# Graph products and transposes as two half-array products per 128 rows, in a four-layer graph network on one core

## The chip, the cores and the metric

The kernel runs on one core of a Trainium2 chip. The metric is the device time of one execution in microseconds (us): 2440.18 us, the median of three runs (2438.67 to 2441.17). All tensors are float32.

## The reference

`x` is 128 batches of 64 nodes of 256 features; `adj` is one 64 x 64 graph, with its own diagonal, for all batches. Four layers follow each other, each of the form `x = layernorm(x + layer(x))`:

```python
# layer 0: normalized graph product, two dense layers with batch norm
agg = einsum('nm,bmd->bnd', A_hat, x)
out = bn(relu(bn(agg @ W1.T + b1)) @ W2.T + b2)
# layer 1: graph product with the scaled Laplacian, attention of 4 heads over the graph, MLP
h  = relu(layernorm(einsum('mn,bnf->bmf', L_norm, x) @ Wc + bc)); x1 = h + x
o  = softmax(mask(q k^T / 8)) v          # q, k, v = x1 @ Wq, Wk, Wv; 4 heads of 64
x2 = layernorm(x1 + o @ Wo + bo); out = layernorm(x2 + gelu(x2 @ W1 + b1) @ W2 + b2)
# layer 2: two graph convolutions, then LSTMs over windows of 1, 2, 3 and 4 nodes
h = relu(adj @ (x @ Wg0 + bg0)); h = relu(adj @ (h @ Wg1 + bg1)); h = lstm_windows(h)
# layer 3: graph attention with additive scores
Wh = x @ W; e = leaky_relu(Wh @ a1 + (Wh @ a2)^T); out = softmax(mask(e)) @ Wh
```

## The kernel before, in words

The 128 batches are cut into 16 blocks of 8 batches. A block is a tile of 128 partitions by 1024 columns and has two layouts. In the row layout (`tm`) the 128 partitions are two batches of 64 nodes, and the columns are 4 such pairs (`t`, `NT` = 4) of 256 features. In the feature layout (`fm`) the partitions are 128 features and the columns are two feature chunks (`c`) of 512 rows each. Everything of eight batches is thus eight squares of 128 x 128.

Work arrives at TensorE (PE) as groups, each of which fills one of four PSUM tiles `ps0` to `ps3`. Such a tile is 128 x 1024 float32 and covers two PSUM banks of 512 columns (`TB`). ScalarE (ACT) or VectorE (DVE) then copies the tile out, often with an addition or an activation in the same instruction, and gives it back. The groups that matter here:

- `aggregate` (L318-328, the product at L322) multiplies a block in the row layout by the graph and leaves it in the feature layout: 8 products, in which the block's square of 128 x 128 is the stationary operand and a 128 x 128 matrix, block diagonal with the graph twice, is the moving one. It is called once per block in layer 0 (`first_block`, with `AhT`), once in layer 1 (`block`, with `LnT`) and twice in layer 2 (`gcn_block`, with `bdAT`): 64 calls.
- `to_fm` (L330, the transposes at L334) and `to_tm` (L336, L340) change the layout with PE transposes of 128 x 128 against `ident`. `block` calls `to_fm` twice, `end_block` calls `to_tm` once, and `last_block` calls each once. The last four blocks are dealt with in two halves there.
- In `block`, the attention: `q` and `k` come from `mm_fm` (L346), `v` from L705; the scores (L730) are 32 products of 64 x 64 by 64 x 64; their softmax is transposed by eight squares (L764); attention times `v` (L778) is again 32 products of 64 x 64 by 64 x 64, whose outputs of head parity `r` go to partition half `r`.
- Dense products: `mm_fm` (L346), `mm_tm` (L358), L566, L835; the LSTM products are at L952, L1024, L1161 and L1163.

The columns of `Wq`, `Wk`, `Wv` are the four heads in turn, 64 each; head 2u + r lies in chunk `u`, half `r`. L609 loads each of these weights with one DMA from SyncE's queue (SP), early in the program.

The order of work on every engine is fixed when the program is written. `flow` (L126) plays a list scheduler: each task is a generator that yields `step(engine, us, ...)` with an estimated time, and `flow` always takes the step that can begin first, by those estimates, with a priority among streams and a count of free PSUM tiles (`PS`) and SBUF tiles (`mem`). The estimate for an aggregation is 1.8, for a transposing group 0.9, for the scores 1.8, for attention times v 2.0, for a dense group 3.45. On the chip each engine then runs its own list in order and waits on semaphores.

Of the kernel before, what the change touches and what calls it, by code (L numbers as in the profile page):

```python
# [33 lines left out]
def kernel(ctx: ExitStack, tc: tile.TileContext, a: dict, out: bass.AP):  # L34
# [267 lines left out]
    def ln_steps_act(y):  # L302
# [10 lines left out]
        for t in range(n):  # L313
            S.activation(  # L314
                y[:, t, :], y[:, t, :], AF.Identity, scale=rs[:, t : t + 1], bias=nm[:, t : t + 1]
            )

    def aggregate(ps, y, mT):  # L318

        for c in range(2):  # L320
            for t in range(NT):
                T.matmul(  # L322
                    ps[:, c, t * P : (t + 1) * P],
                    y[:, t, c * P : (c + 1) * P],
                    mT,
                    start=True,
                    stop=True,
                )

    def to_fm(ps, y):  # L330

        for c in range(2):
            for t in range(y.shape[1]):
                T.transpose(ps[:, c, t * P : (t + 1) * P], y[:, t, c * P : (c + 1) * P], ident)  # L334

    def to_tm(ps, yT):  # L336

        for t in range(ps.shape[1]):
            for c in range(2):
                T.transpose(ps[:, t, c * P : (c + 1) * P], yT[:, c, t * P : (t + 1) * P], ident)  # L340

# [45 lines left out]
    with c0:  # L387
# [135 lines left out]
        def first_block(i):  # L523
# [4 lines left out]
            else:  # L528
                xs = early[i]
            yield step("T", 1.8, ps=1, sl=1)  # L530
            ps = PS.take()
            ag = mem.take()
            aggregate(fm(PS[ps]), tm(mem[xs]), AhT)
            mem.give(xs)
            yield step("V", 1.25, ps=-1)
            aggT = fm(mem[ag])
            V.tensor_copy(aggT, fm(PS[ps]))
            PS.give(ps)
# [69 lines left out]
        for k, w in zip(("Wc", "Wq", "Wk", "Wv", "Wo", "W1", "W2"), (Wc, Wq, Wk, Wv, Wo, W1, W2)):  # L608
            nc.sync.dma_start(w, by_chunk(a[f"L1_gnn_{k}"]))  # L609
        names = ("bc", "g1", "be1", "bo", "g2", "b2", "g3", "be3")  # L610
# [20 lines left out]
    def end_block(i):  # L631
        x = X[i]
        yield step("Q", 6.0, sl=1)
        xin = mem.take()
        nc.sync.dma_start(tm(mem[xin]), x_blk[i])
        yield step("S", 1.4)
        for c in range(2):
            S.activation(
                H[i][:, c, :], H[i][:, c, :], AF.Identity, scale=sc2[:, c : c + 1], bias=sh2[:, c : c + 1]
            )  # L640
        yield step("T", 0.9, ps=1)
        ps = PS.take()
        to_tm(tm(PS[ps]), H[i])
        mark("h", i)
        yield step("V", 1.25, ps=-1)
        V.tensor_tensor(x, tm(PS[ps]), tm(mem[xin]), ALU.add)
        PS.give(ps)
        mem.give(xin)
        yield from ln_steps_act(x)
        mark("end", i)  # L650

    def block(i):
        x = X[i]
        mark("begun", i)
        yield step("T", 1.8, ps=1, sl=1)
        ps = PS.take()
        s_xp = mem.take()
        aggregate(fm(PS[ps]), x, LnT)
        yield step("S", 1.05, ps=-1)
        S.copy(mem[s_xp], PS[ps])  # L660
        PS.give(ps)
# [12 lines left out]

        yield step("T", 0.9, ps=1, sl=1)
        ps = PS.take()
        s_x1 = mem.take()
        to_fm(fm(PS[ps]), y)
        yield step("S", 1.05, ps=-1)
        x1T = fm(mem[s_x1])  # L680
        S.copy(mem[s_x1], PS[ps])  # L681
        PS.give(ps)
# [42 lines left out]
        pq = PS[ps].rearrange("p (r g m) -> p r g m", r=2, g=8)  # L725
        for b in range(8):
            t, s = b // 2, b % 2
            for u in range(2):
                for r in range(2):
                    T.matmul(  # L730
                        pq[s * N : (s + 1) * N, r, 2 * t + u, :],
                        qT[r * N : (r + 1) * N, u, b * N : (b + 1) * N],
                        kT[r * N : (r + 1) * N, u, b * N : (b + 1) * N],
                        start=True,
                        stop=True,
                    )
        for j in qk:
# [20 lines left out]

        yield step("T", 0.9, ps=1, sl=1)
        ps = PS.take()  # L760
        s_a = mem.take()
        pt = PS[ps].rearrange("p (g m) -> p g m", g=8)
        for g in range(8):
            T.transpose(pt[:, g, :], e[:, g, :, :].rearrange("p r m -> p (r m)"), ident)  # L764
        mem.give(s_e)
        yield step("S", 1.05, ps=-1)
        aT = mem[s_a].rearrange("p (g m) -> p g m", g=8)
        S.copy(mem[s_a], PS[ps])
        PS.give(ps)
        yield step("T", 2.0, ps=1, sl=1)  # L770
        ps = PS.take()
        s_o = mem.take()
        po = fm(PS[ps])
        for b in range(8):
            t, s = b // 2, b % 2
            for u in range(2):
                for r in range(2):
                    T.matmul(  # L778
                        po[r * N : (r + 1) * N, u, b * N : (b + 1) * N],
                        v[r * N : (r + 1) * N, b, u, :],  # L780
                        aT[r * N : (r + 1) * N, 2 * t + u, s * N : (s + 1) * N],
                        start=True,
                        stop=True,
                    )
# [14 lines left out]

        yield step("T", 0.9, ps=1, sl=1)  # L800
        ps = PS.take()
        s_x2 = mem.take()
        to_fm(fm(PS[ps]), y)
        yield step("S", 1.4, ps=-1)
        x2T = fm(mem[s_x2])
        for c in range(2):
            S.activation(
                x2T[:, c, :], fm(PS[ps])[:, c, :], AF.Identity, scale=g2c[:, c : c + 1], bias=be2c[:, c : c + 1]
            )
# [393 lines left out]
    def gcn_block(i):  # L1203
        yield step("T", 1.8, ps=1, sl=1)
        ps = PS.take()
        s_a = mem.take()
        aggregate(fm(PS[ps]), X[i], bdAT)
        yield step("Q", 4.0, waits=False)
# [3 lines left out]
        yield step("S", 1.05, ps=-1)  # L1212
        S.copy(mem[s_a], PS[ps])
        PS.give(ps)
# [10 lines left out]
        S.activation(mem[s_h1], mem[s_h1], AF.Relu)  # L1225
        yield step("T", 1.8, ps=1, sl=1)
        ps = PS.take()
        s_a = mem.take()
        aggregate(fm(PS[ps]), h1, bdAT)
        mem.give(s_h1)  # L1230
        yield step("S", 1.05, ps=-1)
        S.copy(mem[s_a], PS[ps])
        PS.give(ps)
# [119 lines left out]
    def last_block(i, t0=0, nt=NT):  # L1353
# [9 lines left out]
        for c in range(2):  # L1363
# [3 lines left out]
            )  # L1367
        yield step("T", 0.9 * r, ps=1)
        ps = PS.take()
        px = tm(PS[ps])[:, :nt, :]  # L1370
        to_tm(px, hb)
        mem.give(s_h)
        mark("read", i)
        yield step("V", 0.1 + 1.2 * r, ps=-1)
        V.tensor_tensor(x, px, x, ALU.add)
        PS.give(ps)
        yield from ln_steps_act(x)

        yield step("T", 0.9 * r, ps=1, sl=1)
        ps = PS.take()  # L1380
        s_xT = mem.take()
        px = fm(PS[ps])[:, :, : nt * P]
        to_fm(px, x)


        yield step("S", 0.3 + 1.1 * r, ps=-1)
        xT = fm(mem[s_xT])[:, :, : nt * P]
        pairs, into = (ap.rearrange("p c (u e k) -> p c u e k", e=2, k=P) for ap in (px, xT))
        S.copy(into[:, :, :, 0], pairs[:, :, :, 0])
        for h in range(2):  # L1390
            S.copy(into[:, :, :, 1, halves[1 - h]], pairs[:, :, :, 1, halves[h]])
        PS.give(ps)
# [243 lines left out]
```

## Time and profile before

| | us |
|---|---|
| median of three runs | 2440.18 |
| the profiled execution | 2439.17 |
| span of its records | 2437.4 |
| PE busy | 2348.3 |
| DVE busy | 1215.1 |
| ACT busy | 1169.9 |
| POOL busy | 566.7 |
| PE, all aggregations (L322) | 130.8 |
| PE, all transposes of `to_fm`, `to_tm` (L334, L340) | 94.4 |
| PE, attention times v (L778) | 33.1 |

The span is what the records of the program cover; the execution's own time is 1.8 us longer. A product of float32 leaves two pairs of records, each a LDWEIGHTS (engine PEld, the stationary operand) and a MATMUL (engine PE, the moving operand): the 128 aggregating products with `AhT` have 256 MATMUL records. A transpose leaves one pair. In a row, `64*64 64x64` says that the stationary operand has 64 partitions by 64 columns and that the output is 64 partitions by 64 columns. [...] The granted clock of PE was 0.983 over the span.

### The profile page before, as it was taken

The numbers are of one execution on the slowest core, as the hardware profiler recorded it, in microseconds if no ns is written. First come the engines' busy times: TensorE is split into PE (matmuls) and PEld (weight loads), VectorE is DVE, ScalarE is ACT, GpSimd is POOL, SyncE is SP. The second block draws the span as 40 slices with busy tenths as digits, with TensorE's granted clock in tenths as the row PEclk, the third lists the DMA queues.
The fourth block names the chain that finished last, engine by engine and source line by source line (L and its number), as shares of the span: only waits on it lengthen the run. The fifth ranks groups of instructions, "written<-read, shape, count | busy, mean of one in ns | idle before, by whom it ended". The sixth has DMA issues, their size and how long they took to land. (4 is left out here: it accounts for less than half of the span.)

```text
span 2437.4 us, 33965 instructions
## 1 busy us (share of the span) xinstructions
PE 2348.3 (96%) x13700; PEld 1798.9 (74%) x13700; DVE 1215.1 (50%) x2864; ACT 1169.9 (48%) x2138; POOL 566.7 (23%) x426
## 2 busy tenths in 40 slices
PE   8999889999999999999999999999999999998997
PEld 5544567766676666676676788899999888887785
DVE  4542377646475345744462433344435444455446
ACT  2255453543444444335544444444444654468766
POOL 0000034222333222422231221222212222122112
PEclk9999989999999999999999999999999999999998
DMA  5110111000000000000010000000001000001111
GB/s 172 44 52 0 40 31 49 27 9 10 1 10 18 10 9 10 1 10 34 20 61 1 18 1 1 1 18 1 1 1 35 1 9 10 18 27 66 40 35 44
DMA packets 40974, 57.47 MB, mean 24 GB/s; under 512 B 4592, under 2 KB 33904, under 8 KB 40816
## 3 DMA queue, kind: packets, MB, share of 16 engines
q1 hardware_dynamic: 39712, 54.22, 6.9%
q8 instruction: 107, 1.75, 0.3%
q10 hardware_dynamic: 1104, 1.08, 0.1%
q14 instruction: 51, 0.42, 0.1%
HBM read 38.52 MB, written 16.78 MB: 23 GB/s over the span
## 5 line engine op out<-in xcount | busy, mean ns | idle before, releaser
L1024 PE MATMUL ps<-x,x 128*128 128x256 f32 x1024 | 248.6, 380 | 0.7 <-DVE t L1092 0.7
L1024 PEld LDWEIGHTS ps<-x,x 128*128 128x128 f32 x1024 | 191.5, 190 | 26.4 <-issue 1.6
L314 ACT ACTIVATE x<-x,ln_nm,ln_rs 128x256 f32<-128x256 f32 x196 | 103.7, 592 | 97.0 <-DVE ln_nm L311 95.5
L1024 PE MATMUL ps<-t,x 128*128 128x256 f32 x576 | 141.0, 379 | 0.0
L308 POOL TENSOR_TENSOR ln_rs<-ln_rs,neghalf 128x4 f32<-128x4 f32 (+1 forms) x72 | 70.5, 980 | 231.1 <-DVE ln_rs L274 217.3
L1024 PEld LDWEIGHTS ps<-t,x 128*128 128x128 f32 x576 | 108.6, 190 | 14.6 <-issue 0.4
L346 PE MATMUL ps<-t,W1T 128*128 128x512 f32 x256 | 115.2, 593 | 0.0
L952 PE MATMUL ps<-h,wL 128*128 128x192 f32 (+2 forms) x504 | 111.6, 375 | 0.0
L952 PEld LDWEIGHTS ps<-h,wL 128*128 128x128 f32 x504 | 79.1, 190 | 27.6 <-issue 26.7
L272 DVE BATCH_NORM_STATS2 ln_st<-x 128x6 f32<-128x256 f32 x256 | 98.2, 404 | 0.5
L1100 ACT ACTIVATE t<-t,bih 128x512 f32<-128x512 f32 (+2 forms) x63 | 41.0, 652 | 107.6 <-DVE t L1090 105.9
L952 PE MATMUL ps<-h,x 128*128 128x256 f32 x384 | 86.8, 379 | 0.0
L964 ACT ACTIVATE t<-ps,bih 128x512 f32<-128x512 f32 (+3 forms) x104 | 61.5, 642 | 44.0 <-PE ps L952 43.9
L294 POOL TENSOR_TENSOR ln_rs<-ln_rs,neghalf 128x4 f32<-128x4 f32 x32 | 36.9, 1153 | 188.8 <-DVE ln_rs L274 188.6
L346 PEld LDWEIGHTS ps<-t,W1T 128*128 128x128 f32 x256 | 46.3, 190 | 46.4 <-issue 46.4
L952 PEld LDWEIGHTS ps<-h,x 128*128 128x128 f32 x384 | 72.9, 190 | 10.3 <-issue 0.5
L1083 DVE COPY t<-ps 128x256 f32<-128x256 f32 (+2 forms) x63 | 23.7, 378 | 113.5 <-PE ps L1024 113.5
L273 DVE BATCH_NORM_AGGREGATE ln_mv<-ln_st 128x2 f32<-128x6 f32 x448 | 71.3, 167 | 0.0
L346 PE MATMUL ps<-t,wA 128*128 128x512 f32 x144 | 67.9, 617 | 2.8 <-ACT t L681 2.8
L952 PE MATMUL ps<-t,wL 128*128 128x512 f32 x144 | 64.9, 607 | 2.5 <-ACT t L1250 2.5
L1090 DVE TENSOR_TENSOR t<-ps,t 128x512 f32<-128x512 f32 (+2 forms) x63 | 38.1, 604 | 54.8 <-PE ps L1024 47.9
L1100 ACT ACTIVATE x<-x,bih 128x512 f32<-128x512 f32 (+2 forms) x57 | 36.6, 641 | 55.7 <-DVE x L1090 55.4
(692 smaller groups left out, 5688.2 us busy)
## 6 DMA issues: line engine op xcount, KB each, us to landing
t<-in_x_dram SPq DMA_DIRECT2D x26, 512.0 KB, 3.9
xd<-x SPq DMA_DIRECT2D x16, 512.0 KB, 2.6
x<-xd SPq DMA_DIRECT2D x6, 512.0 KB, 3.3
out_dram<-x SPq DMA_DIRECT2D x6, 512.0 KB, 3.0
wL<-in_L_gnn_Wih_dram SPq DMA_DIRECT2D x2, 1024.0 KB, 4.9
h<-in_x_dram SPq DMA_DIRECT2D x4, 512.0 KB, 4.2
x<-in_L_gnn_Whh_dram SPq DMA_DIRECT2D x2, 1024.0 KB, 4.9
t<-xd SPq DMA_DIRECT2D x4, 512.0 KB, 3.3
```

What stands on the lines that cost most here:

```text
L272: V.bn_stats(st[:, t, :], y[:, t, :])
L273: V.bn_aggr(mv[:, t, :], st[:, t, :])
L294: G.tensor_tensor(rs, rs, neghalf[:, :NT], ALU.pow)
L308: G.tensor_tensor(rs, rs, neghalf[:, :n], ALU.pow)
L314: S.activation(y[:, t, :], y[:, t, :], AF.Identity, scale=rs[:, t : t + 1], bias=nm[:, t : t + 1])
L346: T.matmul(ps[:, c, :], w[:, k, (off + c) * P : (off + c + 1) * P], yT[:, k, :], start=(k == 0), stop=(k == nk - 1),)
L952: T.matmul(spread(fm(PS[ps])[:, j, :n], q), WL[p][0][:, k, m], x_of(0, q)[:, k], start=(k == 0), stop=(k == 1),)
L964: S.activation(of(sl)[:, j], fm(PS[ps])[:, j, :n], AF.Tanh if g == 2 else AF.Sigmoid, bias=bias(g, c))
L1024: T.matmul(dst, WS[p][name](k, g), y[:, k], start=first and k == 0, stop=k == 1, skip_group_check=not first)
L1083: V.tensor_copy(y[:, 1, :], v[:, 0, :])
L1090: V.tensor_tensor(y[:, 0:2, :], v[:, 2:4, :], y[:, 0:2, :], ALU.add)
L1100: S.activation(of(act[g])[:, 0], of(act[g])[:, 0], f, bias=bias(g, 0))
```

## The change

The two batches of a square are no longer kept apart by zeros in a 128 x 128 matrix. Each aggregating product becomes two, one per batch: the stationary operand is 64 partitions (one half `h` of `halves`) by 128 columns, the moving one the 64 x 64 graph in the same partitions. The same is done with all transposes, against a 64 x 64 piece of `ident`. The two products of a pair write to the two banks of the PSUM tile (`part`), and the copy out joins them again (`joined` reads the banks in turn in runs of 64 columns, `runs` names the destination in the same shape). In attention times v the four combinations of head parity and `u` go to four different quarters of the array, so that heads 2 and 3 change places in the output; the columns of `Wq`, `Wk` and `Wv` are loaded in that order, which takes three DMAs per weight. The score products come in another order. The estimates of the steps concerned are lowered.

```diff
+    def part(ps, s, g):
+        return ps[:, s * TB + g * N : s * TB + (g + 1) * N]
+    def joined(ps, n=2 * NT):
+        return ps.rearrange("p (s g e) -> p g s e", s=2, e=N)[:, :n]
+    def runs(ap):
+        if len(ap.shape) == 2:
+            return ap.rearrange("p (g s e) -> p g s e", s=2, e=N)
+        return ap.rearrange("p t (c s e) -> p (t c) s e", s=2, e=N)
...
     def aggregate(ps, y, mT):
         for c in range(2):
             for t in range(NT):
-                T.matmul(
-                    ps[:, c, t * P : (t + 1) * P],
-                    y[:, t, c * P : (c + 1) * P],
-                    mT,
-                    start=True,
-                    stop=True,
-                )
+                for s, h in enumerate(halves):
+                    T.matmul(
+                        part(ps, s, c * NT + t),
+                        y[h, t, c * P : (c + 1) * P],
+                        mT[h, h],
+                        start=True,
+                        stop=True,
+                    )
     def to_fm(ps, y):
...
-            for t in range(y.shape[1]):
-                T.transpose(ps[:, c, t * P : (t + 1) * P], y[:, t, c * P : (c + 1) * P], ident)
+            for t in range(n):
+                for s, h in enumerate(halves):
+                    T.transpose(part(ps, s, c * n + t), y[h, t, c * P : (c + 1) * P], ident[h, h])
...
-            yield step("T", 1.8, ps=1, sl=1)
+            yield step("T", 0.95, ps=1, sl=1)
...
-            V.tensor_copy(aggT, fm(PS[ps]))
+            V.tensor_copy(runs(mem[ag]), joined(PS[ps]))
...
+            if k in ("Wq", "Wk", "Wv"):
+                for m, j in ((slice(0, P), slice(0, P)), (slice(P, P + N), slice(P + N, 2 * P)), (slice(P + N, 2 * P), slice(P, P + N))):
+                    nc.sync.dma_start(w[:, :, m], src[:, :, j])
...
-        S.copy(mem[s_xp], PS[ps])
+        S.copy(runs(mem[s_xp]), joined(PS[ps]))
...
-        for b in range(8):
-            t, s = b // 2, b % 2
+        for t in range(NT):
             for u in range(2):
-                for r in range(2):
+                for s in range(2):
+                    b = 2 * t + s
+                    for r in range(2):
...
-        yield step("T", 0.9, ps=1, sl=1)
+        yield step("T", 0.5, ps=1, sl=1)
...
         for g in range(8):
-            T.transpose(pt[:, g, :], e[:, g, :, :].rearrange("p r m -> p (r m)"), ident)
+            for s, h in enumerate(halves):
+                T.transpose(part(PS[ps], s, g), mem[s_e][h, g * P : (g + 1) * P], ident[h, h])
...
-        yield step("T", 2.0, ps=1, sl=1)
+        yield step("T", 1.3, ps=1, sl=1)
...
-                        po[r * N : (r + 1) * N, u, b * N : (b + 1) * N],
-                        v[r * N : (r + 1) * N, b, u, :],
-                        aT[r * N : (r + 1) * N, 2 * t + u, s * N : (s + 1) * N],
+                        po[halves[r ^ u], u, b * N : (b + 1) * N],
+                        v[halves[r], b, u, :],
+                        aT[halves[r], 2 * t + u, s * N : (s + 1) * N],
```

The other copies out of aggregations and transposes change as the two shown do; `to_tm` changes as `to_fm`. In `last_block` the copy after `to_fm`, three ACT instructions before (L1389, L1391), becomes two.

## The prediction

> **What bounds the kernel now.** I read the page first: the busy times and the slices. PE is busy 96% of the span in nearly every slice; VectorE and ScalarE are at half. A change of PE work therefore counts almost in full, and a slower copy out of PSUM mostly doesn't.
>
> ```profile
> PE 2348.3 (96%) x13700; PEld 1798.9 (74%) x13700; DVE 1215.1 (50%) x2864; ACT 1169.9 (48%) x2138; POOL 566.7 (23%) x426
> ...
> PE   8999889999999999999999999999999999998997
> ```
>
> Next came the groups by line and shape, for the paces of the products that the change touches and of those that already use half of the array's rows (busy, then mean of one).
>
> ```profile
> L764 PE MATMUL ps<-ident,t 128*128 128x128 f32 x64 | 8.3, 273 | 0.0
> L778 PE MATMUL ps<-h 64*64 64x64 f32 x64 | 2.1, 220 | 0.0
> L730 PE MATMUL ps<-t,x 64*64 64x64 f32 x64 | 1.2, 222 | 0.0
> ```
>
> With 64 records and both less one record: L778 goes at (2.1 - 0.22) / 63 = 30 ns a record, L730 at (1.2 - 0.22) / 63 = 15.6 ns. The first has two quarters of the array in use, so one quarter starts a record each 59 ns; the second has four, and the same pace per quarter. Quarters thus run side by side, and 59 ns is the price of one record with 64 columns loaded and 64 streamed.
>
> The timeline gives the full-array groups.
>
> ```profile
> 424.50 1.84 PE L905 MATMUL ps<-av,t 128*128 128x1 f32 x16
> ...
> 431.51 1.04 PE L764 MATMUL ps<-ident,t 128*128 128x128 f32 x8
> ...
> 704.26 1.95 PE L322 MATMUL ps<-bdAT,h 128*128 128x128 f32 x16
> ```
>
> The aggregation goes at (1.95 - 0.275) / 15 = 112 ns a record, a transpose at (1.04 - 0.273) / 7 = 110 ns. L905 decides what the change is worth: its products stream one column, against 128 of L322, and still start (1.84 - 0.25) / 15 = 106 ns apart. It isn't the streaming that holds them but the loading of 128 columns of weights. The weight loads of four lines, minimum, median and maximum in ns, say what that load depends on:
>
> ```profile
> L905 PEld LDWEIGHTS ps<-av,t x16: 190/192/192, 424.3 to 426.1; 128*128 128x128 f32 x16
> ...
> L705 PEld LDWEIGHTS ps<-wA,t x576: 132/137/138, 324.9 to 1074.3; 128*64 128x64 f32 x192
> ...
> L778 PEld LDWEIGHTS ps<-h x64: 129/135/135, 354.3 to 356.1; 64*64 64x64 f32 x64
> ...
> L764 PEld LDWEIGHTS ps<-ident,t x64: 139/141/146, 365.9 to 1141.7; 128*128 128x128 f32 x64
> ```
>
> 64 columns take 137 ns from 128 rows and 135 ns from 64: rows don't matter. 128 columns take 192 ns, 55 to 57 ns more. But 128 columns of a transpose (L764) take 141 ns, like 64 of a product.
>
> Last I looked at the borders between groups with the whole array and groups in quarters.
>
> ```profile
> 781.15 0.59 PE L346 MATMUL ps<-t,wB 128*128 128x512 f32 x1
> 781.68 0.27 PE L730 MATMUL ps<-t,x 64*64 64x64 f32 x2
> ...
> 781.68 1.21 PE L730 MATMUL ps<-t,x 64*64 64x64 f32 x64
> 782.82 0.33 PE L334 MATMUL ps<-ident,t 128*128 128x128 f32 x1
> ...
> 661.12 1.21 PE L730 MATMUL ps<-t,h 64*64 64x64 f32 x64
> 662.26 0.38 PE L322 MATMUL ps<-LnT,x 128*128 128x128 f32 x1
> ```
>
> From end to end: L346 ends at 781.74 and the first scores at 781.95, 0.21 us later where 0.06 is their pace: 0.15 lost. The scores end at 782.89 and the next transpose at 783.15, 0.26 against 0.11: 0.15 lost. Where an aggregation follows (662.33 to 662.64) it is 0.31 against 0.11: 0.20 lost. Full-array groups that follow each other lose nothing: L322 above starts 0.43 us after the last 512-column product, which is that product's own pace. So each change of the array's shape empties it and shows the first load: 0.15 us where that load is short (64 columns, or a transpose), 0.20 us where a product loads 128 columns.
>
> **The change part by part.**
>
> Aggregations, 64 groups. Before, 16 records in a row at 112 ns: 1.79 us. After, 32 records in two halves, 16 in each: the stationary operand has 64 rows and still 128 columns, so each half is held by the same load, 16 x 112 ns = 1.79 us. Gain: none. The trace has no half of 64 rows by 128 columns, so the ends are the pace of a 64-column record, 16 x 59 ns = 0.94 us (64 x 0.85 = 54 us gained), and halves that don't overlap at all, 3.58 us (115 us lost). I take no gain, since the row nearest to it, L905, has the same load with less streaming; the loss I give hardly a chance, because L730's four quarters load side by side.
>
> [...]
>
> Transposes, 768 of them, 96 groups of eight (the halves of `last_block` counted as halves). Before 8 x 110 ns = 0.88 us; after 8 in each half at 59 ns = 0.47 us, since their load is short. Gain 96 x 0.41 = 39 us. The ends: this, and no gain, if the short load isn't to be had in half of the rows (8 x 112 = 0.90 us).
>
> Attention times v, 16 groups of 64 records, from two quarters to four: 63 x (30 - 15.6) ns = 0.91 us each, 14.5 us. The scores already go at the pace of four quarters: nothing.
>
> Borders. I counted them in the order in which PE's instructions stand in both programs. Before, the shape of the array changes 151 times, 94 of them into a short load and 57 into a long one: 94 x 0.15 + 57 x 0.20 = 25.5 us. After it changes 340 times, 148 and 192: 60.6 us. Loss 35 us. That the shape of 64 rows by 128 columns costs the same per border as the quarters is taken over from the rows above; at nothing for it the loss would be 0, at twice the price 70.
>
> Copies out. They read the two banks in turn, in runs of 64. The nearest rows: ACT's L1391 (256 columns in runs of 64) takes 392 ns against 365 to 377 for plain 256-column copies (L1062, L1064), so 0.1 us more at most for 1024 columns; DVE's L1242 in runs of 64 takes 678 ns for 512 columns against 688 plain at L1090. 168 copies by 0.1 us are 17 us at worst, hidden behind PE's 96%; without that cover they are lost. The copy in `last_block` loses one instruction (585 + 2 x 392 ns to 2 x 585), 0.2 us of ACT, also hidden.
>
> DMAs. Wq, Wk and Wv take nine issues on SP for three, six more of 0.5 to 1.4 us (L609's rows), 3 to 8 us between 12 and 29 us. Behind them on SP wait the other weights, the `rows` and the load of the eighth block of x, issued at 28.6 us before. PE needs that block only after seven blocks of layer 0, each 1.8 + 2 x 3.4 = 8.7 us, so about 60 us after its start at 8; the weights are first used at 297 us. Cost nothing; at most 8 us if that slack weren't there.
>
> Sum: 35 - 39 - 14.5 = -18.5 us. Profiled span 2437.4 - 18.5 = 2418.9; the execution was 1.8 us longer than its span, and the median of the runs 1.0 above that execution: 2421.7. I predict 2421 us.
>
> **The rivals.**
>
> Aggregations are halved as well. For it: two halves would stream 64 columns each. Against it: L905. Then 2421 - 54 = 2367 us.
>
> Transposes don't get faster, so the change is slower. The place is the load of a transpose in 64 rows: L764 has its 141 ns in a full array, and the program's other transposes of halves (L1450) are written as plain products, which is no proof of either. If the load takes what a product's takes, the 39 us are gone, 1.5 us are lost (8 x 112 ns against 0.88), and some 100 of the borders cost 0.20 instead of 0.15, 5 us: 2421 + 46 = 2467 us. It decides from the point where a transposing pair takes more than about 90 ns, since 96 x 8 x 24 ns eat the 18.5 us.
>
> The fixed order turns bad. `flow` now plans 0.95 us for an aggregation that by my sum takes 1.8 plus two borders, 2.2 us; 64 x 1.2 = 79 us of PE work that ACT's and DVE's lists don't reckon with. Before, its 1.8 matched. PE's waits are now 2437 - 2348 = 89 us. A fifth more of them, 18 us, and the gain is gone; with a third more, 2421 + 30 = 2451 us. Against it: a PE that is later than planned finds its inputs ready.
>
> **How the numbers follow.** From one measurement to the next some 0.2% (4.9 us) can't be told from no change. My forecast has 0.52, with its own range 2405 to 2437 (the gain may shrink or grow by the copies' and waits' 16 us); 0.46 of that is faster by over 0.2%, 0.06 the same. Halved aggregations 0.11, all faster. Transposes without gain 0.10, all slower. The bad order 0.27, between 2430 and 2460: 0.03 faster, 0.09 the same, 0.15 slower. Faster 0.60, same 0.15, slower 0.25. The range 2398 to 2464 leaves out the halved aggregations and about half of the case that ends near 2467.
>
> **What would show it.** In the changed kernel's groups: aggregating records of 64 rows by 128 columns with loads of about 192 ns, 32 of them in 1.9 us or so (at 0.95 us my main step is wrong); transposing loads near 141 ns and 16 records in 0.5 to 0.7 us (at 0.9 the second rival holds); attention times v in 1.2 us. At the borders, 0.15 and 0.20 us. PE waits much over 89 us would speak for the order. The forecast falls if the half of 64 rows by 128 columns needs no emptying of the array, or more than one.

## The result, and the profile after

The changed kernel takes 2455.53 us (median of four runs, 2452.9 to 2455.97) against 2440.2 us: 1.006 times the time before, 95% interval [1.0048, 1.0073]. It is slower by 15 us where 19 us less were forecast. The profiled execution has a span of 2451.1 us against 2437.4.

The page of the changed kernel, busy times and two rows of the slices:

```profile
PE 2341.8 (96%) x15492; PEld 1763.8 (72%) x15492; DVE 1216.3 (50%) x2864; ACT 1173.0 (48%) x2123; POOL 570.7 (23%) x426
...
PE   8999888999999999999999999999999999989997
...
PEclk9999889999999999999999999999999999999998
```

PE is busy 6.5 us less than before and yet the span is 13.7 us longer; PEclk, the granted clock in tenths, falls from 9 to 8 in one slice more (the fifth). Busy time alone doesn't say which of its microseconds were worked at full clock. The next view gives the busy times of the engines and the granted clock by stretches (columns: stretch, its length, then PE, PEld, DVE, ACT, POOL busy with the number of instructions, granted clock, DMA share, GB/s), first the kernel before, then the changed one:

```profile
300.00:450.00 150.00, 137.10 (x1151) 102.36 (x1151) 108.29 (x311) 79.56 (x118) 56.79 (x37) 0.95 0.14 43
```

```profile
300.00:450.00 150.00, 132.01 (x1266) 94.65 (x1268) 109.39 (x293) 76.77 (x112) 56.97 (x36) 0.89 0.15 45
```

In this stretch PE is idle for 18 of 150 us, not 13, and the clock is at 0.89, not 0.95.

The steps of the prediction about single products come next. Weight loads of the changed kernel (minimum, median and maximum in ns; L340 is now the aggregation, L354 `to_fm`, L791 the attention's transposes):

```profile
L340 PEld LDWEIGHTS ps<-AhT,t x512: 182/188/334, 8.3 to 140.6; 64*128 64x128 f32 x171
...
L354 PEld LDWEIGHTS ps<-ident,t x368: 134/139/226, 326.6 to 2359.4; 64*128 64x128 f32 x184
...
L791 PEld LDWEIGHTS ps<-ident,t x144: 134/139/195, 445.3 to 1273.8; 64*128 64x128 f32 x144
```

And its timeline (start and length in us; groups of PE):

```profile
443.62 2.00 PE L340 MATMUL ps<-bdAT,x 64*128 64x64 f32 x32
445.45 0.67 PE L791 MATMUL ps<-ident,t 64*128 64x64 f32 x16
...
455.77 1.16 PE L805 MATMUL ps<-h,h 64*64 64x64 f32 x64
```

A product of 64 rows still loads 128 columns in 188 ns, a transpose in 139. Records overlap: the 16 of L791 above have 223 ns each and lie in 0.67 us. So the pace of a group is its busy time less one record, divided by its records less one. The aggregation goes at (2.00 - 0.27) / 31 = 56 ns a record, which is 112 ns in each half, the pace of before. The transposes go at (0.67 - 0.22) / 15 = 30 ns a record, 60 in each half; attention times v at (1.16 - 0.22) / 63 = 15 ns. All three are the prices of the forecast. What is wrong isn't there.

### The profile page after: what moved, and what is told of

It is laid out like the page before. It is cut to its first block, busy times and chain, and to the rows that moved or that the text cites. A ratio compares the mean times of both kernels' runs of the same rounds, so it can differ in the third digit from the quotient of the medians.

```text
span 2451.1 us, 37589 instructions
## 1 busy us (share of the span) xinstructions
PE 2341.8 (96%) x15492; PEld 1763.8 (72%) x15492; DVE 1216.3 (50%) x2864; ACT 1173.0 (48%) x2123; POOL 570.7 (23%) x426
## 5 line engine op out<-in xcount | busy, mean ns | idle before, releaser
L1055 PE MATMUL ps<-x,x 128*128 128x256 f32 x864 | 212.9, 381 | 1.6 <-DVE x L1114 1.0
L1055 PEld LDWEIGHTS ps<-x,x 128*128 128x128 f32 x864 | 160.6, 190 | 25.2 <-issue 2.0
L1055 PE MATMUL ps<-t,x 128*128 128x256 f32 x704 | 170.0, 380 | 0.0
L1055 PEld LDWEIGHTS ps<-t,x 128*128 128x128 f32 x704 | 132.9, 190 | 18.9 <-issue 0.8
L983 PE MATMUL ps<-h,wL 128*128 128x192 f32 (+2 forms) x456 | 90.5, 352 | 0.0
L272 DVE BATCH_NORM_STATS2 ln_st<-x 128x6 f32<-128x256 f32 x224 | 85.7, 403 | 0.4
L983 PEld LDWEIGHTS ps<-h,wL 128*128 128x128 f32 x456 | 70.1, 190 | 16.9 <-issue 15.8
L983 PE MATMUL ps<-t,wL 128*128 128x512 f32 x168 | 73.7, 594 | 1.2 <-ACT t L1281 0.7
L995 ACT ACTIVATE x<-ps,bih 128x512 f32<-128x512 f32 (+3 forms) x84 | 49.0, 634 | 50.2 <-PE ps L983 50.0
L983 PE MATMUL ps<-x,wL 128*128 128x512 f32 x144 | 62.9, 593 | 0.0
```

What stands on the lines that cost most here:

```text
L272: V.bn_stats(st[:, t, :], y[:, t, :])
L983: T.matmul(spread(fm(PS[ps])[:, j, :n], q), WL[p][0][:, k, m], x_of(0, q)[:, k], start=(k == 0), stop=(k == 1),)
L995: S.activation(of(sl)[:, j], fm(PS[ps])[:, j, :n], AF.Tanh if g == 2 else AF.Sigmoid, bias=bias(g, c))
L1055: T.matmul(dst, WS[p][name](k, g), y[:, k], start=first and k == 0, stop=k == 1, skip_group_check=not first)
```

## Experiments

### A ledger of PE's time

All the runs below are read with one ledger, summed over the records of PE in each profiled execution. *Waits* are the stretches over 0.6 us in which no product streams. *Slow clock* is half of the time, outside those waits, in which the granted clock was at half speed, the start before the first full clock included. *Work* is the rest of the span: what the products, loads and borders take at full clock, and the time ahead of the first product and behind the last one, which differs by at most some 2 us among these kernels. Each kernel stands against the one with the same order of work: before, and for the changed kernel `old_instr_new_order`. The forecast is the sum of the prediction's own prices (0.41 us a transposing group, 0.91 us for v, 0.15 and 0.20 us a border, counted in the instructions of each kernel; for quarters the 54 us of the prediction's other bound).

| kernel | work, forecast | work | waits | slow clock | span |
|---|---|---|---|---|---|
| `only_transposes` | -18.2 | -18.8 | +15.1 | +0.5 | -3.2 |
| `only_attention_v` | -14.5 | -12.7 | +5.2 | -3.9 | -11.5 |
| `transposes_and_v` | -32.7 | -34.4 | +25.1 | +5.7 | -3.6 |
| `only_aggregations` | +21.5 | +12.6 | -3.4 | +16.3 | +25.6 |
| `new_instr_old_order` | -17.8 | -29.5 | +24.0 | +25.9 | +20.4 |
| changed kernel | -18.5 | -27.4 | +21.6 | +16.4 | +10.6 |
| `quarters_and_v` | -52.4 | -52.1 | +33.6 | +10.8 | -7.7 |
| `quarters_v_transposes` | -74.0 | -80.2 | +54.6 | +13.1 | -12.5 |

Before has 87.1 us of waits and 30.6 of slow clock, `old_instr_new_order` 90.5 and 30.4. The prices of the work hold, within 2 us for the transposes, for v and for the quarters with v. With half transposes as well, the quarters' work is 6 us less than priced, and whenever the aggregating halves are in it, the work is 9 to 12 us less; some 3 of these are borders priced too high (see below), the rest stays unexplained. The time is lost in the two columns that the forecast's sum doesn't have.

### Instructions and order, crossed

The first run has the changed instructions with the estimates of before, and so before's order; the second the reverse.

```diff
-            yield step("T", 0.95, ps=1, sl=1)      # new_instr_old_order, from the changed kernel
+            yield step("T", 1.8, ps=1, sl=1)
...
-            yield step("T", 1.8, ps=1, sl=1)       # old_instr_new_order, from before
+            yield step("T", 0.95, ps=1, sl=1)
```

> The changed kernel's instructions with the estimates of the kernel before, so that the work stands on every engine in the order it had before the change. Theory O (the instructions save what the sum said, about 18 us, and the new order of work costs about 32): 2422 us, 2415 to 2430. Theory I (the new instructions themselves cost the 15 us, by waits that the sum did not see, such as slower copies out of the two banks): 2455 us, 2450 to 2460.

> The instructions of the kernel before with the estimates of the changed kernel, so that its work stands in the changed kernel's order. Theory O: 2440 + 32 = 2472 us, 2460 to 2480. Theory I: the order is harmless, 2440 us within 5.

Measured: 2459.53 us, ratio 1.008 [1.0066, 1.0093], for the new instructions in the old order; 2440.69 us, 1.0002 [0.9993, 1.0011], for the old instructions in the new order. The loss comes with the new instructions in either order; the order that the lowered estimates make costs the old instructions nothing.

Two more runs ask whether better estimates would help: the changed kernel with 2.15 for an aggregation, 0.8 for transposes and 1.3 for v, and before with 1.85 for 1.8.

```diff
-            yield step("T", 0.95, ps=1, sl=1)
+            yield step("T", 2.15, ps=1, sl=1)
```

> The changed kernel with estimates near what its groups take with their borders: 2.15 for an aggregation instead of 0.95, 0.8 for a transposing group instead of 0.5; attention times v stays at 1.3. Theory E (the order is bad because the estimates were too short): 2422 us, 2415 to 2430. Theory L (any new order is a draw, the one before was a lucky one): anywhere between 2420 and 2465, and no better than the changed kernel by rule.

> The kernel before with 1.85 instead of 1.8 as the estimate of an aggregation, nothing else; the planner makes another order of it from the second block of layer 1 on. Theory E: an estimate that is 3% off costs next to nothing, 2440 us within 5. Theory L: the time moves by 5 to 30 us although no instruction differs, most likely up.

Measured: 2484.28 us, 1.0173 [1.0159, 1.0187], and 2453.07 us, 1.0056 [1.0043, 1.0069]. An estimate moved by 3% costs before 13 us, nearly as much as the whole change does, and truer estimates made the changed kernel 29 us slower. The order behaves like a draw here, and an edit of a few microseconds has to be compared in one and the same order. From here on all kernels have the estimates of before.

### One part alone

```diff
-                T.matmul(ps[:, c, t * P : (t + 1) * P], y[:, t, c * P : (c + 1) * P], mT, start=True, stop=True)
+                for s, h in enumerate(halves):              # only_aggregations
+                    T.matmul(part(ps, s, c * NT + t), y[h, t, c * P : (c + 1) * P], mT[h, h], start=True, stop=True)
...
-                T.transpose(ps[:, c, t * P : (t + 1) * P], y[:, t, c * P : (c + 1) * P], ident)
+                for s, h in enumerate(halves):              # only_transposes
+                    T.transpose(part(ps, s, c * n + t), y[h, t, c * P : (c + 1) * P], ident[h, h])
...
-                        po[r * N : (r + 1) * N, u, b * N : (b + 1) * N],
+                        po[halves[r ^ u], u, b * N : (b + 1) * N],   # only_attention_v
```

> The kernel before, in its order, with the aggregations alone in half-array products. The borders of about 52 visits cost 20 us at full clock by the prediction's prices, and nothing is gained: 2460 us if the clock is granted as before. Theory C (products in 64 rows don't keep the clock up): 2470 to 2480 us, with a later first full clock (24 us instead of 11) and 15 us or more of granted clock lost. Theory W (what was lost are waits of other engines, the clock is a coincidence): 2460 us within 5 and the clock as before.

> The kernel before, in its order, with the transposes alone in half-array products. The sum says 39 us gained and some 20 to 25 us of borders lost: 2422 to 2428 us at an unchanged clock. Theory C: 2430 to 2445 us, with clock lost near 290 us and 2420 us of the span, where transposes stand in a row. Theory W: 2425 us.

> The kernel before, in its order, with attention times v over four quarters, the new order of the scores and the permuted weight loads alone. The sum says 14.5 us gained: 2426 us. Theory C agrees, since no product gets smaller: 2426 us within 5, clock as before. If PE's waits take half of any gain here: 2433 us.

> Half transposes and attention times v over four quarters, aggregations full, order of before. If the two gains are independent: 3.3 + 6.7 below 2440.2, 2430 us. If the waits that each turns into are the same waits: 2433 to 2437. If they only pay together, below 2427. The loss to the clock should stay between 33 and 45 us if it is the aggregating halves that lower it, and go above 50 if it is PE's waits.

Measured: aggregations 2464.93 us, 1.0102 [1.0089, 1.0116]; transposes 2436.91, 0.9988 [0.9979, 0.9997]; attention times v 2433.45, 0.997 [0.9959, 0.9981] (its runs lie between 2427.66 and 2436.86, and the profiled one is the lowest); transposes and v together 2438.19, 0.9991 [0.9982, 1.0001]. The aggregations cost 25 us. Transposes and v, which save PE 34 us of work, save 2 us of time, which can't be told from nothing.

Where the 34 us go, the waits of PE show (engine, line waited for: us in total, times, longest). Before:

```profile
PE ps L358 <- ACT h L964: 3.5, 1, 3.5
PE ps L334 <- DVE t L1222: 3.4, 1, 3.4
PE ps L340 <- ACT h L964: 3.4, 1, 3.4
```

`transposes_and_v`:

```profile
PE ps L350 <- DVE t L1249: 4.8, 1, 4.8
PE ps L357 <- ACT h L991: 4.3, 1, 4.3
PE ps L375 <- ACT h L991: 4.1, 1, 4.1
...
PE ps L357 <- ACT h L660: 3.5, 6, 1.1
PE ps L979 <- ACT t L1277: 3.4, 2, 2.9
PE ps L363 <- DVE h L1249: 3.2, 1, 3.2
```

Three known waits have grown (`to_tm` is L340 before and L357 here, `to_fm` L334 and L350, `mm_tm` L358 and L375), and new ones stand beside them. The copies out of PSUM, which read the two banks in turn, aren't why: on DVE the copy behind layer 0's aggregation takes 1224 ns before (L537) and 1225 in the changed kernel (L558), on ACT the one behind layer 1's 1012 in both (L660, L686). The timeline shows one of these, where layer 1 begins and `to_tm` takes what ACT has just scaled. Before, then `transposes_and_v`; the bracket is the idle time before a group and what ended it:

```profile
282.64 0.45 PE L340 MATMUL ps<-ident,h 128*128 128x128 f32 x1 [0.61 <-ACT h L638]
283.25 1.75 PE L340 MATMUL ps<-ident,h 128*128 128x128 f32 x7 [0.17 <-ACT h L638]
285.37 0.48 PE L340 MATMUL ps<-ident,h 128*128 128x128 f32 x1 [0.36 <-ACT h L638]
286.33 5.72 PE L340 MATMUL ps<-ident,h 128*128 128x128 f32 x29 [0.48 <-DVE x L646]
293.17 0.49 PE L322 MATMUL ps<-LnT,x 128*128 128x128 f32 x2 [1.13 <-ACT x L314]
```

```profile
285.42 0.37 PE L357 MATMUL ps<-ident,h 64*128 64x64 f32 x2 [0.73 <-ACT h L660]
286.04 1.01 PE L357 MATMUL ps<-ident,h 64*128 64x64 f32 x14 [0.25 <-ACT h L660]
288.15 2.08 PE L357 MATMUL ps<-ident,h 64*128 64x64 f32 x32 [1.11 <-ACT h L660]
290.97 0.37 PE L357 MATMUL ps<-ident,h 64*128 64x64 f32 x2 [0.74 <-ACT h L660]
291.68 1.12 PE L357 MATMUL ps<-ident,h 64*128 64x64 f32 x16 [0.33 <-ACT h L660]
293.09 0.69 PE L357 MATMUL ps<-ident,h 64*128 64x64 f32 x8 [0.29 <-ACT h L660]
294.39 0.80 PE L336 MATMUL ps<-LnT,x 128*128 128x128 f32 x2 [0.61 <-ACT x L314]
```

In the longest group a square takes 5.72 / 29 = 0.197 us before and 2.08 / 16 = 0.130 here; over the 37 or 38 squares ahead of the first aggregation (L322, L336) that is 2.5 us less work. The waits in brackets add up to 2.75 us before and to 4.06 here. From the first transpose to the first aggregation it is 10.5 us and 9.0: ACT's scaling sets much of the pace, and half of the saving is spent waiting for it.

### What raises the granted clock

In `new_instr_old_order` the trace's first record of a full clock stands at 24.0 us, in before at 10.9. The timeline of PE's start shows what that does, before:

```profile
7.97 5.21 PE L322 MATMUL ps<-AhT,t 128*128 128x128 f32 x32 [0.45 <-DVE AhT L441]
...
13.16 2.03 PE L322 MATMUL ps<-AhT,t 128*128 128x128 f32 x16
```

and `new_instr_old_order`:

```profile
8.34 7.09 PE L340 MATMUL ps<-AhT,t 64*128 64x64 f32 x64 [0.44 <-DVE AhT L462]
...
15.87 3.68 PE L340 MATMUL ps<-AhT,t 64*128 64x64 f32 x32
```

The third aggregation takes 3.68 us, which is half speed, where before it already has full speed (2.03). PE is busy without a break in both. Two probes follow: before, with added dummy products in bursts. A burst repeats one kind of product; it begins after 9.5 to 9.7 us of rest, at half clock (0.50), except the first of each probe and those that directly follow full products.

```diff
+    rest()
+    full(100)            # 128x128, 128 columns streamed
+    rest()
+    rows(60)             # pairs of 64-row halves, 64 columns streamed
+    rest()
+    quarters(120)
...
```

> The kernel before, followed by about 600 us of rests (PE idle for some 17 us) and bursts of products whose results nobody reads: full products, pairs of halves of 64 rows, one half alone, four quarters, two diagonal quarters, two halves of columns, full transposes, half transposes, and then full products followed at once by halves, two quarters, full transposes, half transposes. The time is not of interest, the granted clock is. Theory C: it rises to full within 10 us in the full products and the four quarters, stays at half for the whole burst in pairs of halves, in one half and in two quarters, and falls back within 10 to 20 us where those follow full products. Theory W: it rises in all bursts alike after the same time.

> The kernel before, followed by rests of some 17 us and bursts: full products with 128 columns streamed, full products with 64, pairs of halves with 64, with 128 and with 256 columns streamed, one half with 256, full products with one column, one quarter, four quarters. Only the granted clock is of interest. Theory D (what counts is the share of time in which a product streams; a load of 128 columns that streams 64 fills half of it): full products with 64 and with one column stay at half, pairs of halves rise with 128 and 256 columns, one half and one quarter rise too. Theory R (64 rows do not count): pairs of halves stay at half whatever they stream, and full products with 64 columns rise.

The first probe, bursts by stretches (granted clock third from the end); in this order full products, pairs of halves, one half alone, two diagonal quarters, and halves directly behind full products:

```profile
2435.00:2452.00 17.00, 17.00 (x155) 17.00 (x154) 0.16 (x1) 1.63 (x4) 0.52 (x1) 1.00 0.14 48
2465.00:2488.00 23.00, 23.00 (x220) 23.00 (x218) 0.00 (x0) 0.00 (x0) 0.00 (x0) 0.50 0.01 1
2500.00:2524.00 24.00, 24.00 (x115) 24.00 (x114) 0.00 (x0) 0.00 (x0) 0.00 (x0) 0.50 0.00 1
...
2576.00:2586.00 10.00, 10.00 (x352) 10.00 (x347) 0.00 (x0) 0.00 (x0) 0.00 (x0) 1.00 0.02 5
...
2686.00:2708.00 22.00, 22.00 (x396) 22.00 (x398) 0.00 (x0) 0.00 (x0) 0.00 (x0) 1.00 0.01 2
```

The second probe; full products with 64 columns streamed, pairs of halves with 64, with 128 and with 256, one half alone with 256, a single quarter, four quarters:

```profile
2470.00:2502.00 32.00, 32.00 (x151) 31.91 (x150) 0.00 (x0) 0.00 (x0) 0.00 (x0) 0.50 0.00 1
2514.00:2546.00 32.00, 32.00 (x302) 31.84 (x300) 0.00 (x0) 0.00 (x0) 0.00 (x0) 0.50 0.00 1
2564.00:2575.00 11.00, 11.00 (x202) 11.00 (x200) 0.00 (x0) 0.00 (x0) 0.00 (x0) 1.00 0.01 1
2592.00:2603.00 11.00, 11.00 (x104) 9.73 (x102) 0.00 (x0) 0.00 (x0) 0.00 (x0) 1.00 0.01 1
2626.00:2674.00 48.00, 48.00 (x114) 37.08 (x113) 0.00 (x0) 0.00 (x0) 0.00 (x0) 0.50 0.00 0
...
2731.00:2753.00 22.00, 22.00 (x210) 22.00 (x209) 0.00 (x0) 0.00 (x0) 0.00 (x0) 0.50 0.00 1
2768.00:2780.00 12.00, 7.58 (x487) 7.17 (x476) 0.00 (x0) 0.00 (x0) 0.00 (x0) 1.00 0.02 5
```

PE counts as fully busy in every burst that stayed at half clock. It isn't the shape: pairs of halves raised the clock when they streamed 128 columns (after 6.2 us) or 256 (after 2.9). It isn't streaming without a break: one half alone with 256 columns streams all the time (51.56 us for 120 records at half clock, thus 0.215 us a record at full, which is 256 columns at the 0.84 ns below), and the clock stayed at half for its 52 us. It isn't the share of the array's cells: two diagonal quarters use half of the cells, one in each half of the rows, and raised the clock after 5.6 us. What fits all the bursts is the share of the array's rows, over the time, in which data stream: about half or less didn't raise the clock (at the 0.43 us of a 512-column product, L346 before, thus an estimated 0.84 ns a column, 64 columns stream for 54 of a half's 112 ns; full products with 64 likewise; one half alone has half of the rows), nine tenths or more, such as the quarters' 54 of 59 ns, raised it after 2.7 to 6.2 us. A clock that was full already wasn't lowered by the sparse halves within 22 us (1.00 from 2686 to 2708 us), where they followed full products without a break.

### The same halves, streaming more

`halves_streamed_twice` is `new_instr_old_order` with the 64 columns streamed twice; the second copy is overwritten by the next product. `layer0_full` is `new_instr_old_order` with layer 0's aggregations full.

```diff
-                        part(ps, s, c * NT + t),
+                        twice(ps, s, c * NT + t),                  # 128 output columns, 64 for the last
                         y[h, t, c * P : (c + 1) * P],
-                        mT[h, h],
+                        bc_mid(mT[h, h], 2 if c * NT + t < 7 else 1),
...
-            aggregate(PS[ps], tm(mem[xs]), AhT)                    # layer0_full
+            aggregate_full(fm(PS[ps]), tm(mem[xs]), AhT)
```

> All instructions of the change in the order of before, as new_instr_old_order (2459.53 us), but every aggregating half streams its 64 columns twice (the second copy is overwritten by the next product), so that the array streams nearly all the time and not half of it; loads, borders, copies and order stay. Theory that the granted clock follows the share of rows and time in which data stream: the halves keep their pace (a load of 128 columns binds: 16 records in a half in 1.8 to 1.9 us), the first full clock comes at about 11 to 14 us and not at 24, the time lost to the clock falls from 67.6 to 45 to 55 us, and the run takes 2437 to 2450 us. Rival, that the clock falls because PE waits longer and not because of what the halves stream: the loss to the clock stays at 62 or more and the run takes 2455 to 2463. If the halves become bound by streaming, L322's time end to end grows above 150 us and the run is slower than 2463.

> As new_instr_old_order (2459.53 us), but layer 0 keeps the full 128x128 aggregation; layers 1 and 2 have the halves. If the halves in the first 25 us only hold the clock down there, the first full clock is back at 10.9 us, which gives back about 6.5 us, and some 32 borders at 0.15 to 0.20 go, 5 to 6 us: 2446 to 2449 us. If the loss of clock lies in layers 1 to 3, the loss to the clock stays within 5 of 67.6 less those 6.5, that is 56 to 66. If the early half clock is made up for by later waits, the run takes 2453 or more.

Measured: 2477.07 us, 1.0151 [1.0134, 1.0167], and 2452.26 us, 1.005 [1.0035, 1.0065]. The start of `halves_streamed_twice`:

```profile
8.37 5.09 PE L344 MATMUL ps<-AhT,t 64*128 64x128 f32 x64 [0.44 <-DVE AhT L466]
...
13.70 2.00 PE L344 MATMUL ps<-AhT,t 64*128 64x128 f32 x32
```

With the same loads, the same halves and the same PE list the first full clock comes at 11.1 us, not 24.0, and the third aggregation has full speed. At the start the cause is shown: what the halves stream. With full products there it comes at 12.0 us, and 7 us of the time come back.

Later in the run, in `only_aggregations`, halves went with half clock too, where a wait of 1.01 us stands ahead of them. In this place two aggregations with `LnT` come behind a wait for ACT and one with `bdAT` follows. Before, then `only_aggregations`:

```profile
893.32 3.84 PE L322 MATMUL ps<-LnT,x 128*128 128x128 f32 x32 [1.16 <-ACT x L964]
897.00 1.95 PE L322 MATMUL ps<-bdAT,x 128*128 128x128 f32 x16
```

```profile
912.00 5.49 PE L338 MATMUL ps<-LnT,x 64*128 64x64 f32 x64 [1.01 <-ACT x L980]
917.27 3.63 PE L338 MATMUL ps<-bdAT,x 64*128 64x64 f32 x32
```

Before, the granted clock is 1.00 throughout. In `only_aggregations`, after a shorter wait, it is 0.50 from 914 to 924 us, and the aggregation with `bdAT` takes nearly twice as long. `new_instr_old_order` and `halves_streamed_twice` both have a wait of 2.5 us there; the aggregation with `bdAT` in each:

```profile
917.88 3.63 PE L340 MATMUL ps<-bdAT,x 64*128 64x64 f32 x32
```

```profile
923.42 1.95 PE L344 MATMUL ps<-bdAT,x 64*128 64x128 f32 x32
```

Half clock lasts 13.7 us in the first and 3.4 in the second.

But the time forecast for `halves_streamed_twice` was 2437 to 2450 us, and it is 18 us slower than with the clock held down. It has 50 us more waits than before (137.3 us) and 43 us of slow clock. The first new wait lies right behind the start (waits of that kernel):

```profile
DVE rows L653 <- DMA be<-in_L_gnn_be_dram: 11.7, 1, 11.7
```

```profile
PE ps L493 <- DVE eM L506: 9.8, 2, 7.6
```

DVE stands 11.7 us for `be2` (3.7 before), which SP issues behind the weights of layer 1 and their six added DMAs; behind it in DVE's list is the scaling of `eM` that PE waits for, 7.6 us in one go, and the clock falls to half again. In `new_instr_old_order` PE was so late at this place that the same DVE instruction waited 0.23 us. The held-down clock had hidden the late load.

The loads of `rows` and `be2` were then issued ahead of the weights, with PE's list unchanged:

```diff
+        load_rows(rows, [a[f"L1_gnn_{k}"] for k in names])
+        nc.sync.dma_start(be2, a["L1_gnn_be2"].partition_broadcast(P))
         for k, w in zip(("Wc", "Wq", "Wk", "Wv", "Wo", "W1", "W2"), (Wc, Wq, Wk, Wv, Wo, W1, W2)):
...
-        load_rows(rows, [a[f"L1_gnn_{k}"] for k in names])
-        nc.sync.dma_start(be2, a["L1_gnn_be2"].partition_broadcast(P))
```

> halves_streamed_twice (2477.07 us) with the loads of the eight rows and of be2 issued before the weights of layer 1; PE's list is the same. There VectorE stood 11.7 us at 25 us for the transfer of be2, behind which the scaling of eM and with it PE waited 7.6 us, and half clock followed. If the six added issues on SP's queue cause that wait and it is what swallowed the restored clock of the start: the wait is gone, the later DVE milestones come 6 to 11 us earlier, and the run takes 2464 to 2471 us. If the other engines' chains take the time again later: within 3 us of 2477.

> quarters_v_transposes (2426.69 us) with the loads of the eight rows and of be2 issued before the weights of layer 1; PE's list is the same. There VectorE waited 9.5 us for be2 and PE 4.0 us for the eM behind it. If that wait reaches the end: 2419 to 2423 us. If the gain turns into other waits, since PE's order is made for slower groups: 2425 to 2428.

Measured: 2475.41 us, 1.0149 [1.0135, 1.0162], and 2431.24 us, 0.9958 [0.9944, 0.9971]. This tells nothing of the question: the addition that uses `be2` moved up in DVE's list together with the load, so DVE still waits 11.2 and 12.6 us, only earlier, and PE behind it 8.2 and 5.2. What the wait costs at the end of the run isn't known.

### Quarters

If a product loads only 64 columns, the prediction's other bound of 54 us applies. Each aggregating product becomes four.

```diff
-                for s, h in enumerate(halves):
-                    T.matmul(part(ps, s, c * NT + t), y[h, t, c * P : (c + 1) * P], mT[h, h], start=True, stop=True)
+                for f in halves:
+                    for s, h in enumerate(halves):
+                        T.matmul(part(ps, s, c * NT + t)[f], y[h, t, c * P + f.start : c * P + f.stop], mT[h, h], start=True, stop=True)
```

> The kernel before, in its order, with attention times v over four quarters and with each aggregating product as four of 64 rows by 64 columns, so that 64 columns are loaded for 64 streamed; transposes are full. By the sum 64 x 0.83 us are gained on aggregations, 14.5 us on v, and 16 us of borders lost: 51 us, 2389 us. Theory D (the clock needs products that stream most of the time, and quarters do): the clock rises as before, at 11 to 13 us, and the time is 2389 to 2415 us, the upper end if PE's waits take half of the gain. Theory R (any product in 64 rows holds the clock back): the clock rises after 20 us again, 2420 to 2440 us.

> The same with the transposes in halves as in the changed kernel, thus the whole change with its aggregations in quarters instead of halves. By the sum another 39 us gained and 17 lost at borders: 2368 us; from what the transposes brought alone, 3 us of 18, rather 2385 to 2410. Theory D: clock lost as in the kernel before within 10 us. Theory R: 2420 to 2445 us with 20 us or more of clock lost.

Measured: 2431.44 us, 0.9962 [0.995, 0.9975], with full transposes; 2426.69 us, 0.9949 [0.9935, 0.9963], with half transposes as well. The second is the fastest kernel of the study and beats both kernels: it is 29 us faster than the change. Its first full clock comes at 12.8 us; four quarters stream nine tenths of the time, as in the probe. And yet of 80 us of work less, 12 arrive: 55 became waits, 13 slow clock. Both times lie above what was expected of a clock that rises early, 2389 to 2415 and 2385 to 2410 us.

## Why the prediction was wrong

*Right by its own steps.* The aggregations gain nothing, since 128 columns are loaded (112 ns a half, as L905's row said). Of the 54 us of the other bound the halves gain none; the quarters, which load 64 columns, gain nearly all in their own groups (64 records at 15 ns, 0.96 us, against 1.79). The transposes gain 0.41 us a group, v 0.91. Medians at the borders are 0.15 us into a transpose and 0.20 into a whole-array product that loads 128 columns. Into the aggregating halves, which the sum priced at 0.20, they are 0.14 (at the aggregation shown above the last dense product ends at 443.69 us and the first pair of halves at 443.94, and 0.11 is its pace); over some fifty such borders that is 3 us. The work went down by 27 us where the sum had 18.5. That the copies out cost nothing was right as well.

*The step that failed* is the premise of its first paragraph, that PE is busy 96% and "a change of PE work therefore counts almost in full", and with it the sum "2437.4 - 18.5 = 2418.9". It keeps two terms at their values of before: PE's waits and the granted clock. Measured in the order of the changed kernel, the waits grew by 21.6 us and the slow clock took 16.4 more, so that -27.4 became +10.6.

- *Waits.* 96% is an average. Where PE saved time it came up, group by group, against operands that ACT and DVE hadn't finished. `transposes_and_v`, with 34.4 us of work less, 25.1 us of waits more and the aggregations untouched, shows this by itself. The four per cent that PE waited before already showed which chains were nearly as long as PE's: L358 and L340 behind ACT L964, L334 behind DVE L1222.
- *Clock.* The granted clock was no term of the sum. Where aggregations are made of halves the slow clock is 43 to 62 us, without them (before, `only_transposes`, `only_attention_v`, `transposes_and_v`) 27 to 36. `only_aggregations` shows that the halves do this by themselves: its waits are 3.4 us shorter in sum than before's, and its slow clock is 16.3 us longer, some 6 of them at the start and 5 at the place shown at 914 us. Longer waits go with slow clock too: `transposes_and_v` has 5.7 us more, and the quarters, which raise the clock, have 41 to 50 us of it. In the changed kernel both come together, and how its 16.4 us divide stays open.

*The third rival* named the right size for the wrong reason. Its "a third more" waits and 2451 us are close to what came (24% more than with the old instructions in the same order). But it blamed the estimates in `flow`, and `old_instr_new_order` (1.0002) and `new_instr_old_order` (1.008) clear them: the waits come with before's order too. Truer estimates don't remove them either: `new_instr_true_estimates` has 133 us of waits and 62 of slow clock. Whether some other order would let more of the saved time arrive isn't shown. That the measured time lies within the 2398 to 2464 us of the prediction is owed to this rival's share and, with its cause wrong, to luck.

*The second rival*, transposes without gain, falls: they gain in work all that was forecast.

*The DMAs* were priced at nothing because PE needs the weights late. That overlooked `be2` behind them and the DVE instruction that waits for it. This wait is 3.7 us before and 0.5 in the changed kernel, so the price came out right; but only because PE was late itself.

## What to carry to other kernels

A saving on an engine that is busy 96% is worth its microseconds only where the inputs of the groups that follow are ready (`transposes_and_v` saved 34 us of work and 2 us of time): list the waits that it already has, and the slack of the groups next to the edit, before counting the saving in full. Put the granted clock into the sum as a term, above all for small products that load longer than they stream, as the halves here, with some 54 ns of streaming in a pace of 112. And compare edits in one order of work, with the estimates held: here a 3% nudge of one estimate moved the time by 13 us, the whole change by 15.

## What the runs showed of the hardware

- Full PE activity alone did not raise the granted clock. Pairs of 64-row halves that stream 64 columns behind loads of 128 left it at 0.50 for 34.4 us, and so did full products with 64 columns or with one; the same halves with 128 columns raised it after 6.2 us and with 256 after 2.9. Once it was full (1.00), 22 us of the sparse halves directly behind full products didn't lower it; with a wait of 1.01 us ahead of them, in `only_aggregations`, it fell to 0.50 for 10 us, where full products behind 1.16 us kept it.
- Float32 transposes raised the clock too, in the first probe: after 2.7 us as full squares, after 3.7 as halves.
- A change of the array's shape cost 0.15 us ahead of a transpose, 0.14 ahead of aggregating halves and 0.20 ahead of a whole-array product that loads 128 columns; the changed kernel has 340 such changes. At a change the first load of the new shape starts 0.07 us before the last record of the old one ends; within one shape a load starts 0.22 to 0.38 us before the end of the record ahead of it (medians of the kernels before and after).
